# A two-block bottleneck network on 16 images: four first convolutions ahead of the first attention, weights prepared without ScalarE, and a new order of the 3x3 groups

## The chip, the cores and the metric

The kernel runs on one core of one Trainium2 chip. The metric is the device time of one execution in microseconds. "The time" of a kernel below is the median of its timed executions; a profile is one single execution, taken by the hardware profiler.

## The reference

The input is 16 images of 1024 channels and 32x32 pixels, in float32. Two residual bottleneck blocks follow each other. The first has local self-attention in its middle, the second a 3x3 convolution, computed by the Winograd method (inputs and weights are transformed, so that fewer multiplications are needed). Cut to what matters:

```python
# block 0
h = relu(bn(conv1x1(x, w_conv1)))                 # 1024 -> 256: "first convolution"
q = relu(bn(conv1x1(h, wq)))                      # "projections"
k = relu(bn(conv1x1(h, wk)))
v = bn(conv1x1(h, wv))
kp = unfold3x3(k) + pos                           # 9 taps, 32 heads of 8 channels
attn = softmax(einsum('bgdhw,bgdkhw->bgkhw', q, kp), axis=taps)
a = relu(bn(einsum('bgdkhw,bgkhw->bgdhw', unfold3x3(v), attn)))
x = relu(bn(conv1x1(a, w_conv3)) + x)             # 256 -> 1024: "third convolution"
# block 1
h = relu(bn(conv1x1(x, w1)))                      # 1024 -> 256: "reduction"
h = relu(bn(conv3x3(h, w2)))                      # "3x3 groups" (Winograd)
x = relu(bn(conv1x1(h, w3)) + x)                  # 256 -> 1024: "expansion"
```

## The kernel before

TensorE multiplies, ScalarE evicts PSUM (copies finished sums out of the accumulators, with scale, bias and relu), VectorE does the attention (products, sums over taps, weighted terms) and the Winograd transforms. The weights that stay the same are prepared once at the start and stored to device memory: two scaled 1x1 weights and the transformed 3x3 weights.

```python
def winograd_weights():
    for m in range(NW):                      # two halves
        ...                                  # three loads of u2t, issued by ScalarE
        for i, row in enumerate((g[0], mid[0], mid[1], g[2])):
            ...
            spread(lambda j: row[:, j, :], lambda j: u[:, j, :], WID)      # VectorE
            nc.scalar.activation(u[:, 0, :], row[:, 0, :], AF.Identity)
            nc.scalar.activation(u[:, 3, :], row[:, 2, :], AF.Identity)
            nc.scalar.dma_start(uw[i][:, m], u)
        yield
```

The attention of a later image is a generator, `side`, that is advanced a little after each piece of TensorE work; the number in `side.leave(us)` says how many us of VectorE work are let out there.

```python
def cycle(b, conv3):
    for o in conv3.chunks(take("w3", b), attended.pop(b), nothing):   # third convolution
        ...                                                           # residual loads
        side.leave(3.0)
    along(reduce_one(b), 3.0)                                         # reduction
    forms = transform(b)
    ...
    if 0 < b and b + 2 < B:                                           # first convolution of b + 2
        for c in first_conv(b + 2): ...
    for at, _ in enumerate(winograd_conv(b, forms, early)): ...       # 3x3 groups
    if more:
        for at in project(b + 2):                                     # projections of b + 2
            ...
            side.leave(3.0)
        side.start(attend(b + 2))
    ...
    for o in last.chunks(...):                                        # expansion
        nc.scalar.dma_start(out[b, ...], xr.pop((b, o)))
        if o >= BEHIND:                                               # BEHIND = 3
            load_residual(b + 1, o - BEHIND)
        if o == 4 and following:
            finish_attended(b + 1)                                    # relu of the attention's result
        side.leave(3.0)
```

So one image's turn is: third convolution, reduction, first convolution of the image two ahead, 3x3 groups, projections of the image two ahead, expansion. The 3x3 groups are sixteen pieces of eight matmuls; four accumulator tiles i = 0 to 3 get four pieces each, and ScalarE copies a tile's sum out after `first(i)` and again after `second(i)`, before the next piece may add to that tile.

```python
for part, i in (
    (first, 0), (third, 0), (first, 1), (second, 0), (third, 1), (last, 0), (second, 1),
    (first, 2), (third, 2), (last, 1), (second, 2), (first, 3), (last, 2), (second, 3),
    (third, 3), (last, 3),
):
```

Three times a piece follows on the same tile directly after a piece whose sum is being copied out: `(third, 0)` after `(first, 0)`, `(third, 2)` after `(first, 2)` and `(third, 3)` after `(second, 3)`. Everywhere else at least one piece of another tile lies between.

Of the kernel before, what the change touches and what calls it, by code (L numbers as in the profile page):

```python
# [13 lines left out]
P = 128  # L14
# [11 lines left out]
XSTREAM = 4  # L26
NJ = 4
# [34 lines left out]
def sa_bottleneck_kernel(ctx: ExitStack, tc: tile.TileContext, x, w1t, wqkvt, w3t, u1t, u2t, u3t, params, out):  # L62
# [17 lines left out]
    def load_x(b, c):  # L80

        if b < B:
            t = xpool.tile([P, HW], F32, tag="x", name=f"x_{b}_{c}")
            nc.gpsimd.dma_start(t, x[b, c * P : (c + 1) * P, :])
            xs[b, c] = t
# [17 lines left out]
    def fetch(name, b):  # L103

        t = wpool.tile([P, 2048], F32, tag="w", name=f"{name}_{b}")
        if name[0] == "U":
            i = int(name[1])
            nc.sync.dma_start(t, uw[i].rearrange("p m j o -> p (m j o)"))
            ready.append((name, b, t.rearrange("p (m j o) -> p m j o", m=NW, j=NU)))
            return  # L110
        if name in ("w3", "u3"):
            nc.sync.dma_start(t, ws[name == "u3"].rearrange("p n o -> p (n o)"))
            ready.append((name, b, t.rearrange("p (n o) -> p n o", n=NW)))
            return
        src, n = {"w1": (w1t, WID), "wqkv": (wqkvt, 3 * WID), "u1": (u1t, WID)}[name]
        chunks = src.shape[0] // P
        view = t[:, : chunks * n].rearrange("p (c n) -> p c n", n=n)
        nc.sync.dma_start(view, src.rearrange("(c p) n -> p c n", p=P))
        ready.append((name, b, view))
# [76 lines left out]
    def scaled_weights(which, src, scale):  # L196
        t = ppool.tile([P, NW, C], F32, tag="t", name="scaled")
        nc.scalar.dma_start(t, src.rearrange("(n p) o -> p n o", p=P))
        diag = ppool.tile([P, 2 * HW], F32, tag="t", name="diag")[:, :C]
        nc.vector.tensor_tensor(  # L200
            diag.rearrange("p (o m) -> p o m", m=P),
            eye.unsqueeze(1).to_broadcast([P, NC, P]),
            scale.unsqueeze(2).to_broadcast([P, NC, P]),
            ALU.mult,
        )
        row = psum.tile([P, C], F32, tag="ps", name="row")
        for half in range(2):
            nc.tensor.matmul(row[:, halves(half)], ones, diag[:, halves(half)], start=True, stop=True)
        for n in range(NW):
            nc.vector.tensor_tensor(t[:, n, :], t[:, n, :], row, ALU.mult)  # L210
        nc.scalar.dma_start(ws[which], t)
# [12 lines left out]
    def winograd_weights():  # L224
        for m in range(NW):
            g = []
            for i in range(3):
                t = rpool.tile([P, HW], F32, tag="r", name="g")[:, : 3 * WID]
                nc.scalar.dma_start(t, u2t[m * P : (m + 1) * P, i * 3 * WID : (i + 1) * 3 * WID])
                g.append(t)  # L230
            mid = [rpool.tile([P, HW], F32, tag="r", name="mid")[:, : 3 * WID] for _ in range(2)]
            spread(lambda i: g[i], lambda i: mid[i - 1], 3 * WID)
            for i, row in enumerate((g[0], mid[0], mid[1], g[2])):
# [4 lines left out]
                nc.scalar.activation(u[:, 0, :], row[:, 0, :], AF.Identity)  # L238
                nc.scalar.activation(u[:, 3, :], row[:, 2, :], AF.Identity)
                nc.scalar.dma_start(uw[i][:, m], u)  # L240
# [182 lines left out]
    def logits(b):  # L423
# [38 lines left out]
        se = apool.tile([P, JPIX], F32, tag="se", name="se")  # L462
# [82 lines left out]
    def winograd_conv(b, forms, early):  # L545
# [8 lines left out]
        def small(name, bufs=2):  # L554
            return zpool.tile([P, NW * TILES], F32, tag=name, name=name, bufs=bufs)
# [31 lines left out]
        def second(i):  # L587
# [3 lines left out]
            diffs[i] = small("d", 1)  # L591
# [25 lines left out]
        for part, i in (  # L617
            (first, 0), (third, 0), (first, 1), (second, 0), (third, 1), (last, 0), (second, 1),
            (first, 2), (third, 2), (last, 1), (second, 2), (first, 3), (last, 2), (second, 3),
            (third, 3), (last, 3),  # L620
        ):
            part(i)
            yield part, i
# [46 lines left out]
    BEHIND = 3  # L670

    def cycle(b, conv3):
# [9 lines left out]
        if 0 < b and b + 2 < B:  # L682
# [8 lines left out]
        more = b + 2 < B  # L691
        for at, _ in enumerate(winograd_conv(b, forms, early)):
            if not more and at in (12, 14):
                last.seed()
        if more:
            for at in project(b + 2):
                if at == ("bnk", 0):
                    finish_winograd(b)
                elif at == ("q", 1):
                    side.finish()  # L700
                    last.seed()
                elif at == ("bnv", 0):
                    last.seed()
                side.leave(3.0)
            side.start(attend(b + 2))
        else:
            side.finish()
            finish_winograd(b)
        following = last_conv(b + 1) if b + 1 < B else None
        for o in last.chunks(  # L710
# [5 lines left out]
            if o == 4 and following:  # L716
                finish_attended(b + 1)
            side.leave(3.0)
        return following


    queue += [("w1", 0), ("wqkv", 0), ("w1", 1), ("w1", 2), ("wqkv", 1)]
    for b in range(B):
        queue += [("w3", b), ("u1", b)]
        if 0 < b and b + 2 < B:
            queue.append(("w1", b + 2))
        queue += [(f"U{i}", b) for i in range(NU)]
        if b + 2 < B:
            queue.append(("wqkv", b + 2))
        queue.append(("u3", b))  # L730
# [7 lines left out]
    forms = winograd_weights()  # L738
    for c in first_conv(0):
        if c in (2, 4):  # L740
            next(forms)
    scaled_weights(0, w3t, col("L0_conv_bn3_s", 0, NC))
    scaled_weights(1, u3t, bn_inv[:, 2 * NW : 2 * NW + NC])
# [5 lines left out]
    along(first_conv(2), 3.4)  # L749
    conv3 = last_conv(0)  # L750
    for at in project(1):
        if at == ("q", 1):
            side.finish()
            conv3.seed()
        elif at == ("bnv", 0):
            conv3.seed()
        side.leave(3.4)
# [44 lines left out]
```

## Time and profile before

| | before |
|---|---|
| time, median of 3 runs | 2855.01 us (2852.85 to 2861.91) |
| profiled execution | span 2844.2 us, timed 2845.9 us |
| TensorE busy | 92% of the span, mean granted clock 0.969 |
| start to the first third convolution | 229.0 us |
| image 0, image 1, image 2 | 183.8, 166.4, 164.6 us |
| images 3 to 13, together | 1827.6 us (166.1 each) |
| images 14 and 15 to the end | 272.8 us |

The image rows are read from the trace: an image begins at the first matmul of its third convolution and ends at that of the next image. They cover the whole span, so two kernels can be compared stretch by stretch, and the differences add up exactly.

The first is the chain that ended last, around the end of the first attention (columns: start us, duration us, what):

```profile
212.74 4.00 DMA a<-acc
...
218.03 12.36 DMA a<-a
```

The attention's result is stored in 4.0 us and loaded again in the other layout in 12.4 us. The second is what TensorE waited for over images 3 to 13 (total us, times, longest us):

```profile
PE ps L299 <- ACT ps L290: 24.5, 18, 4.1
PE ps L568 <- ACT m L582: 15.8, 22, 0.7
PE ps L568 <- ACT m L590: 8.5, 11, 1.0
```

The first row is the expansion or third convolution waiting for its accumulator to be seeded with the residual; the other two are 3x3 groups (line 568) that wait for ScalarE to copy their tile out: 33 waits in 11 images, three per image.

### The profile page before, as it was taken

To read this page: it belongs to the slowest core of one execution; us is meant where nothing else is said; L and a number is where in the kernel's file an instruction comes from. 1 tells how busy PE (TensorE), PEld (TensorE's weight loads), DVE (VectorE), ACT (ScalarE), POOL (GpSimd) and SP (SyncE) were. 2 spreads that over 40 slices of the span, in tenths; PEclk is the share of its full clock that TensorE was granted. 3 is DMA by queue.
4 is the path that set the end of the run, shared out by engine and by line. 5 is a ranking of instruction groups with operands and counts; after the bars stand their busy time and mean duration, and the time that the engine had idled before them with its cause. 6 is when DMAs were issued, how large, how long until landed. Compare 5 with 4: busy or idle time off the path is not lost.

```text
span 2844.2 us, 19171 instructions
## 1 busy us (share of the span) xinstructions
PE 2626.0 (92%) x7048; PEld 1331.0 (47%) x7048; DVE 1945.2 (68%) x1693; ACT 949.3 (33%) x947; POOL 199.1 (7%) x363
## 2 busy tenths in 40 slices
PE   5767869999999999999999999999999999999888
PEld 2323524545454454545445454544545454454535
DVE  3676697496685949668593976859496685948703
ACT  1122231432515244251524425152442515143233
POOL 1100000000001000010100001010000101000000
PEclk8988979999999999999999999999999999999899
DMA  8843462645738264573826457382645738163332
GB/s 281 286 138 113 139 226 87 244 165 176 266 116 316 86 236 174 173 276 115 316 90 239 164 176 279 107 322 91 243 167 174 274 114 322 67 242 145 126 133 96
DMA packets 185358, 533.23 MB, mean 187 GB/s; under 512 B 12720, under 2 KB 102832, under 8 KB 164528
## 3 DMA queue, kind: packets, MB, share of 16 engines
q1 hardware_dynamic: 113152, 233.33, 23.8%
q0 software_dynamic: 50688, 220.75, 21.7%
q10 hardware_dynamic: 21424, 77.92, 6.9%
q8 instruction: 57, 0.93, 0.1%
q14 instruction: 37, 0.30, 0.0%
HBM read 372.03 MB, written 159.91 MB: 187 GB/s over the span
## 4 chain that ended last, share of the span: by engine, by line
PE 74%; DMA 17%; DVE 5%; ACT 2%; issue 1%; ACTq 0%; POOL 0%; SPq 0%; DVEq 0%; POOLq 0%
PE ps L268 30%; PE ps L299 17%; PE ps L568 16%; PE ps L351 10%; DMA u<-in_u1t_dram 8%; DMA bnv<-vh 3%; DMA r<-in_x_dram 3%; DVE term L478 2%; DVE acc L490 2%; PE ps L399 1%; DMA g<-in_u2t_dram 1%; ACT m L582 1%; DMA a<-a 1%; ACT ps L290 1%; ACT vh L361 0%
## 5 line engine op out<-in xcount | busy, mean ns | idle before, releaser
L430 DVE TENSOR_TENSOR prod<-qc,bnk 128x2048 f32<-128x2048 f32 x144 | 329.0, 2285 | 400.4 <-DMA qc<-q 400.3
L299 PE MATMUL ps<-a,w 128*128 128x512 f32 x1024 | 455.3, 605 | 78.2 <-ACT a L503 44.3
L568 PE MATMUL ps<-v,U 128*128 128x256 f32 x2048 | 468.3, 388 | 47.3 <-ACT m L582 23.0
L299 PE MATMUL ps<-h,u 128*128 128x512 f32 x1024 | 453.3, 603 | 42.2 <-ACT ps L290 35.6
L268 PE MATMUL ps<-x,w 128*128 128x512 f32 x1024 | 445.8, 596 | 28.7 <-DMA x<-in_x_dram 28.7
L568 PEld LDWEIGHTS ps<-v,U 128*128 128x128 f32 x2048 | 391.8, 193 | 128.4 <-ACT m L582 36.8
L268 PE MATMUL ps<-r,u 128*128 128x512 f32 x1024 | 442.1, 592 | 0.0
L299 PEld LDWEIGHTS ps<-a,w 128*128 128x128 f32 x1024 | 196.1, 193 | 337.2 <-issue 235.7
L351 PE MATMUL ps<-h,wqkv 128*128 128x512 f32 x768 | 337.0, 595 | 0.0
L299 PEld LDWEIGHTS ps<-h,u 128*128 128x128 f32 x1024 | 197.5, 194 | 294.8 <-issue 233.1
L268 PEld LDWEIGHTS ps<-x,w 128*128 128x128 f32 x1024 | 195.8, 191 | 275.6 <-issue 246.1
L268 PEld LDWEIGHTS ps<-r,u 128*128 128x128 f32 x1024 | 194.6, 190 | 244.9 <-issue 244.9
L290 ACT ACTIVATE ps<-r 128x1024 f32<-128x1024 f32 x256 | 261.8, 1023 | 134.8 <-DMA r<-in_x_dram 73.5
L490 DVE TENSOR_TENSOR acc<-acc,term 128x2048 f32<-128x2048 f32 x128 | 293.4, 2292 | 4.4
L478 DVE TENSOR_TENSOR term<-e,bnv 128x2048 f32<-128x2048 f32 x128 | 292.5, 2285 | 0.9
L351 PEld LDWEIGHTS ps<-h,wqkv 128*128 128x128 f32 x768 | 145.0, 190 | 183.9 <-issue 171.0
L308 ACT ACTIVATE r<-ps,par 128x1024 f32<-128x1024 f32 x128 | 142.2, 1111 | 174.2 <-PE ps L299 174.2
L433 DVE TENSOR_TENSOR prod<-prod 128x1024 f32<-128x1024 f32 x144 | 176.4, 1225 | 5.0
L308 ACT ACTIVATE r<-ps,bn_sh 128x1024 f32<-128x1024 f32 x128 | 141.7, 1107 | 85.0 <-PE ps L299 85.0
L322 ACT ACTIVATE h<-ps,par 128x1024 f32<-128x1024 f32 x32 | 38.4, 1204 | 393.2 <-PE ps L268 392.7
L537 DVE TENSOR_TENSOR v<-tv 128x512 f32<-128x512 f32 x256 | 160.0, 687 | 2.2
L532 DVE TENSOR_TENSOR tv<-vh 128x1088 f32<-128x1088 f32 x64 | 82.3, 1286 | 112.5 <-ACT vh L520 112.3
(83 smaller groups left out, 1286.1 us busy)
## 6 DMA issues: line engine op xcount, KB each, us to landing
x<-in_x_dram POOLq DMA_DIRECT2D x128, 512.0 KB, 3.8
r<-in_x_dram POOLq DMA_DIRECT2D x128, 512.0 KB, 8.1
U<-uw SPq DMA_DIRECT2D x64, 1024.0 KB, 4.8
out_dram<-r ACTq DMA_DIRECT2D x128, 512.0 KB, 8.1
bnk<-kp SPq DMA_DIRECT2D x32, 680.0 KB, 4.1
bnk<-bnk POOLq DMA_DIRECT2D x16, 1360.0 KB, 9.6
bnv<-vh SPq DMA_DIRECT2D x32, 680.0 KB, 10.4
bnv<-bnv POOLq DMA_DIRECT2D x16, 1360.0 KB, 9.7
```

Source lines behind the costliest of these rows:

```text
L268: nc.tensor.matmul(ps[n][:, halves(half)], wt[:, c, n * P : (n + 1) * P], src[:, halves(half)], start=(c == 0), stop=(c == NC - 1),)
L290: nc.scalar.activation(ps, xr[self.b, len(self.ahead)], AF.Identity)
L299: nc.tensor.matmul(ps[:, halves(half)], wt[:, n, o * P : (o + 1) * P], src[:, n, halves(half)], start=False, stop=(n == NW - 1), skip_grou ...
L308: nc.scalar.activation(xr[self.b, o], ps, RELU, bias=self.shift(o), scale=1.0)
L351: nc.tensor.matmul(ps[:, halves(half)], wqkv[:, m, at : at + P], h[:, m, halves(half)], start=(m == 0), stop=(m == NW - 1),)
L430: nc.vector.tensor_tensor(by_row(t), by_row(qc), kc[:, :, i : i + JROWS, j : j + W], ALU.mult)
L433: nc.vector.tensor_add(t[:, 0:4], t[:, 0:4], t[:, 4:8])
L478: nc.vector.tensor_tensor(by_row(dst), rows(e[:, k, :]).unsqueeze(1).to_broadcast([P, HEAD_DIM, JROWS, W]), vc[:, :, i : i + JROWS, j : j ...
L490: nc.vector.tensor_add(acc, acc, t)
L532: nc.vector.tensor_tensor(t, vh[:, :, i0 : i0 + 2 * NT - 1 : 2, :], vh[:, :, i1 : i1 + 2 * NT - 1 : 2, :], op)
L537: nc.vector.tensor_tensor(v[:, j].rearrange("p n (r w) -> p n r w", w=NT), t[:, :, :, j0 : j0 + 2 * NT - 1 : 2], t[:, :, :, j1 : j1 + 2 * ...
L568: nc.tensor.matmul(sums[i][:, at, n * TILES : (n + 1) * TILES], u[:, m, j, n * P : (n + 1) * P], v[:, j, m, :], start=(start and m == 0 an ...
```

## The change

The intent: fill TensorE while the first attention runs, by moving image 3's first convolution ahead of it, and with it take work out of image 1; prepare weights without ScalarE in the way; let no 3x3 group wait for a copy; load each residual one chunk behind the store that frees its buffer. In images 0 and 1 the projections of images 2 and 3 now come after the expansion instead of before it. Cut to its core:

```diff
+AHEAD = 4
     def winograd_weights():
...
-                nc.scalar.dma_start(t, u2t[...])
+                nc.sync.dma_start(t, u2t[...])
...
-                nc.scalar.activation(u[:, 0, :], row[:, 0, :], AF.Identity)
-                nc.scalar.activation(u[:, 3, :], row[:, 2, :], AF.Identity)
-                nc.scalar.dma_start(uw[i][:, m], u)
+                nc.vector.tensor_copy(u[:, 0, :], row[:, 0, :])
+                nc.vector.tensor_copy(u[:, 3, :], row[:, 2, :])
+                nc.sync.dma_start(uw[i][:, m], u)
...
         for part, i in (
-            (first, 0), (third, 0), (first, 1), (second, 0), (third, 1), (last, 0), (second, 1),
-            (first, 2), (third, 2), (last, 1), (second, 2), (first, 3), (last, 2), (second, 3),
-            (third, 3), (last, 3),
+            (third, 0), (first, 0), (third, 1), (second, 0), (first, 1), (last, 0), (second, 1),
+            (third, 2), (first, 2), (last, 1), (third, 3), (first, 3), (second, 2), (second, 3),
+            (last, 2), (last, 3),
         ):
...
-    BEHIND = 3
+    BEHIND = 1
...
-        if 0 < b and b + 2 < B:
+        if has_first(b):                       # AHEAD <= b + 2 < B
             for c in first_conv(b + 2):
...
-        more = b + 2 < B
+        more, late = b + 2 < B, b + 2 < AHEAD
...
-        if more:
-            for at in project(b + 2): ...
-            side.start(attend(b + 2))
+        if more and not late:
+            projections()                      # project(b + 2), then side.start(attend(b + 2))
...
         for o in last.chunks(...):
...
+        if late:
+            projections()
+            finish_attended(b + 1)
...
-    queue += [("w1", 0), ("wqkv", 0), ("w1", 1), ("w1", 2), ("wqkv", 1)]
+    queue += [("w1", 0), ("wqkv", 0), ("w1", 1), ("w1", 2), ("wqkv", 1), ("w1", 3)]
...
     along(first_conv(1), 3.4)
     along(first_conv(2), 3.4)
-    ...                                        # project(1) with side.leave(3.4)
+    along(project(1), 3.4)
+    along(first_conv(3), 3.4)
+    side.finish()
```

Beside these, the first four images' input loads go out from ScalarE instead of GpSimd, the scaled weights come before the Winograd weights and both before the first convolution, and the new group order gets a second buffer for its differences, paid for by letting the softmax sum share the maximum's buffer. The first `w1` is loaded in eight pieces instead of one.

More of the change, by code (lines that the diff above doesn't have):

```diff
@@ L83, in load_x @@
             t = xpool.tile([P, HW], F32, tag="x", name=f"x_{b}_{c}")
-            nc.gpsimd.dma_start(t, x[b, c * P : (c + 1) * P, :])
+            (nc.scalar if b < AHEAD else nc.gpsimd).dma_start(t, x[b, c * P : (c + 1) * P, :])
             xs[b, c] = t
@@ L117, in fetch @@
         view = t[:, : chunks * n].rearrange("p (c n) -> p c n", n=n)
-        nc.sync.dma_start(view, src.rearrange("(c p) n -> p c n", p=P))
+        src = src.rearrange("(c p) n -> p c n", p=P)
+        if b == 0 and name == "w1":
+            for c in range(chunks):
+                nc.sync.dma_start(view[:, c], src[:, c])
+        else:
+            nc.sync.dma_start(view, src)
         ready.append((name, b, view))
@@ L194, in sa_bottleneck_kernel, with scale_row @@
     )
-    def scaled_weights(which, src, scale):
-        t = ppool.tile([P, NW, C], F32, tag="t", name="scaled")
-        nc.scalar.dma_start(t, src.rearrange("(n p) o -> p n o", p=P))
+    def scale_row(scale):
         diag = ppool.tile([P, 2 * HW], F32, tag="t", name="diag")[:, :C]
@@ L208, in scaled_weights @@
             nc.tensor.matmul(row[:, halves(half)], ones, diag[:, halves(half)], start=True, stop=True)
+        return row
+    def scaled_weights(which, src, row):
+        t = ppool.tile([P, NW, C], F32, tag="t", name="scaled")
+        nc.sync.dma_start(t, src.rearrange("(n p) o -> p n o", p=P))
         for n in range(NW):
             nc.vector.tensor_tensor(t[:, n, :], t[:, n, :], row, ALU.mult)
-        nc.scalar.dma_start(ws[which], t)
+        nc.sync.dma_start(ws[which], t)
     def spread(g, dst, shape):
@@ L228, in winograd_weights @@
                 t = rpool.tile([P, HW], F32, tag="r", name="g")[:, : 3 * WID]
-                nc.scalar.dma_start(t, u2t[m * P : (m + 1) * P, i * 3 * WID : (i + 1) * 3 * WID])
+                nc.sync.dma_start(t, u2t[m * P : (m + 1) * P, i * 3 * WID : (i + 1) * 3 * WID])
                 g.append(t)
@@ L461, in logits @@
         yield 3.0
-        se = apool.tile([P, JPIX], F32, tag="se", name="se")
+        se = apool.tile([P, JPIX], F32, tag="mx", name="se")
         tree(ALU.add, se)
@@ L552, in winograd_conv, with small @@
         us, sums, firsts, diffs = {}, {}, {}, {}
-        def small(name, bufs=2):
-            return zpool.tile([P, NW * TILES], F32, tag=name, name=name, bufs=bufs)
+        def small(name):
+            return zpool.tile([P, NW * TILES], F32, tag=name, name=name, bufs=2)
         def by_tile(ap):
@@ L590, in second @@
             nc.scalar.activation(both, sums[i][:, 0], AF.Identity)
-            diffs[i] = small("d", 1)
+            diffs[i] = small("d")
             nc.vector.scalar_tensor_tensor(diffs[i], firsts[i], 2.0, both, ALU.mult, ALU.subtract)
@@ L690, in cycle, with projections @@
         last = expand_last(b)
-        more = b + 2 < B
+        more, late = b + 2 < B, b + 2 < AHEAD
         for at, _ in enumerate(winograd_conv(b, forms, early)):
-            if not more and at in (12, 14):
+            if (late or not more) and at in (12, 14):
                 last.seed()
-        if more:
+        def projections():
             for at in project(b + 2):
-                if at == ("bnk", 0):
+                if at == ("bnk", 0) and not late:
                     finish_winograd(b)
@@ L700, in cycle @@
                     side.finish()
-                    last.seed()
-                elif at == ("bnv", 0):
+                    if not late:
+                        last.seed()
+                elif at == ("bnv", 0) and not late:
                     last.seed()
@@ L705, in cycle @@
             side.start(attend(b + 2))
+        if more and not late:
+            projections()
         else:
-            side.finish()
             finish_winograd(b)
@@ L715, in cycle, with has_first @@
                 load_residual(b + 1, o - BEHIND)
-            if o == 4 and following:
+            if o == 4 and following and not late:
+                side.finish() if not more else None
                 finish_attended(b + 1)
             side.leave(3.0)
-        return following
-    queue += [("w1", 0), ("wqkv", 0), ("w1", 1), ("w1", 2), ("wqkv", 1)]
+        if late:
+            projections()
+            finish_attended(b + 1)
+        return following
+    def has_first(b):
+        return AHEAD <= b + 2 < B
+    queue += [("w1", 0), ("wqkv", 0), ("w1", 1), ("w1", 2), ("wqkv", 1), ("w1", 3)]
     for b in range(B):
         queue += [("w3", b), ("u1", b)]
-        if 0 < b and b + 2 < B:
+        if has_first(b):
             queue.append(("w1", b + 2))
         queue += [(f"U{i}", b) for i in range(NU)]
+        after = [("u3", b)]
         if b + 2 < B:
-            queue.append(("wqkv", b + 2))
-        queue.append(("u3", b))
+            after.insert(1 if b + 2 < AHEAD else 0, ("wqkv", b + 2))
+        queue += after
     load_x(0, 0)
@@ L737, in sa_bottleneck_kernel @@
     more_weights()
-    forms = winograd_weights()
-    for c in first_conv(0):
-        if c in (2, 4):
-            next(forms)
-    scaled_weights(0, w3t, col("L0_conv_bn3_s", 0, NC))
-    scaled_weights(1, u3t, bn_inv[:, 2 * NW : 2 * NW + NC])
+    scales = [scale_row(col("L0_conv_bn3_s", 0, NC)), scale_row(bn_inv[:, 2 * NW : 2 * NW + NC])]
+    scaled_weights(0, w3t, scales[0])
+    scaled_weights(1, u3t, scales[1])
+    for _ in winograd_weights():
+        pass
+    along(first_conv(0), 0.0)
     along(project(0), 0.0)
@@ L749, in sa_bottleneck_kernel @@
     along(first_conv(2), 3.4)
+    along(project(1), 3.4)
+    along(first_conv(3), 3.4)
+    side.finish()
     conv3 = last_conv(0)
-    for at in project(1):
-        if at == ("q", 1):
-            side.finish()
-            conv3.seed()
-        elif at == ("bnv", 0):
-            conv3.seed()
-        side.leave(3.4)
+    for _ in range(2):
+        conv3.seed()
     finish_attended(0)
```

## The prediction

> **What bounds the kernel now.** I read the page first, then busy time by stretches cut at the starts of the third convolutions, then the timelines of TensorE, VectorE and the issuing engines inside the stretches where TensorE is not full.
>
> The page: span, busy row, and TensorE's row of the 40 slices.
>
> ```profile
> span 2844.2 us, 19171 instructions
> PE 2626.0 (92%) x7048; PEld 1331.0 (47%) x7048; DVE 1945.2 (68%) x1693; ACT 949.3 (33%) x947; POOL 199.1 (7%) x363
> PE   5767869999999999999999999999999999999888
> ```
>
> TensorE is full from the seventh slice (about 430 us) on, apart from the tail. The change leaves its arithmetic alone, so it can win only in the head, in the few us that TensorE loses per image, and in the tail. Busy time by stretch: start-up, first attention, images 0 and 1, one steady image (columns: length, PE, PEld, DVE, ACT, POOL busy, clock, DMA share, GB/s).
>
> ```profile
> 0.00:98.00 98.00, 67.20 (x146) 28.38 (x147) 27.06 (x61) 17.72 (x27) 12.64 (x25) 0.90 0.81 280
> 98.00:229.00 131.00, 72.67 (x169) 31.17 (x167) 110.58 (x80) 19.38 (x16) 17.35 (x32) 0.79 0.62 213
> 229.00:413.00 184.00, 147.34 (x377) 75.37 (x378) 133.99 (x115) 54.43 (x55) 6.80 (x12) 0.86 0.38 133
> 413.00:579.00 166.00, 162.94 (x440) 82.74 (x440) 105.95 (x91) 58.40 (x58) 11.59 (x21) 0.99 0.54 193
> 1245.00:1411.00 166.00, 162.97 (x445) 82.91 (x444) 122.36 (x105) 59.17 (x59) 12.66 (x23) 1.00 0.56 200
> ```
>
> From 98 to 229 us VectorE is busy for 110.6 of 131 us: the first attention sets the pace. From 229 to 413 us image 0 takes 184 us for 147 of matmuls. Image 1 and the steady images, each with one first convolution inside, take 166. The timelines say what each stretch waits for.
>
> ```profile
> 71.49 2.35 DVE L210 TENSOR_TENSOR scaled<-scaled,row 128x1024 f32<-128x1024 f32 x2 [7.58 <-DMA scaled<-in_u3t_dram]
> 75.53 1.47 SPq L375 DMA_DIRECT2D bnk<-kp  x2
> 98.17 2.29 DVE L430 TENSOR_TENSOR prod<-qc,bnk 128x2048 f32<-128x2048 f32 x1 [24.33 <-DMA qc<-q]
> 167.36 1.22 DVE L449 TENSOR_TENSOR tree<-e 128x1024 f32<-128x1024 f32 x1 [18.32 <-ACT e L460]
> ...
> 228.96 2.08 PE L299 MATMUL ps<-a,w 128*128 128x512 f32 x2 [43.64 <-ACT a L503]
> 292.13 3.75 PE L568 MATMUL ps<-v,U 128*128 128x256 f32 x8 [4.08 <-issue]
> ...
> 1496.55 12.35 PE L568 MATMUL ps<-v,U 128*128 128x256 f32 x56 [0.69 <-ACT m L582]
> 1509.65 10.63 PE L568 MATMUL ps<-v,U 128*128 128x256 f32 x48 [0.75 <-ACT m L582]
> 1521.03 3.72 PE L568 MATMUL ps<-v,U 128*128 128x256 f32 x16 [0.75 <-ACT m L590]
> ...
> 1576.29 3.70 PE L299 MATMUL ps<-a,w 128*128 128x512 f32 x8 [1.42 <-ACT ps L290]
> ...
> 2671.48 26.27 PE L299 MATMUL ps<-h,u 128*128 128x512 f32 x56 [3.25 <-ACT h L630]
> ```
>
> The reader should see: weight preparation ends near 74 us and only then are k and q stored, so attention starts at 98; its exponential comes 18.3 us late, because ScalarE has it queued behind the first convolution that ends at 162.5; TensorE waits 43.6 us for the result. In a steady image the 3x3 groups lose 0.69+0.75+0.75 = 2.2 us, and seeding the sums with residuals a few us more. The waits of TensorE over 745 to 2400 us (ten images) sum to 22.4 us for seeds and 14.3+7.7 = 22.0 us for the groups: 2.2 us each per image.
>
> **What the Trainium skill says.** "TensorE: Matmul & The Clock Gate", Part 1, "What's actually happening": after an idle window of about 3.4 us the array falls to half clock and needs about as much busy time to recover. The trace agrees: clock 0.79 in the stretch with the 43.6 us wait, 1.00 in the steady one. "VectorE: DVE Perf Modes", the perf-mode tier table: float32 copies and tensor_scalar run at twice the rate of tensor_tensor. Here a 128x256 tensor_scalar took 0.28 us and a tensor_tensor 0.42, which sizes the new copies. "DMA: Bandwidth & Descriptors", "Issuing engines are not separate DMA queues": moving an issue saves sequencer time, not transfer time. The trace agrees: DMA is 0.81 busy in the first 98 us, whoever issues.
>
> **The change part by part.**
>
> Weight preparation. ScalarE is freed of 16 copies of about 0.4 us and of all waits behind them; VectorE gets 16 copies of 0.28, about 5 us in all with gaps. The chain itself stays serial, now on SyncE, which also stores k and q: whatever stands behind it waits as before. Link by link, with this trace's durations: the first scaled weight lands behind 5.7 MB of other loads at about 300 GB/s, near 20 us; its multiply 2.4; the second load 8 and multiply 2.4 (33.5); three loads of 3x3 weights about 10 (44.5); one half on VectorE 8.6+2.6 = 11.2 (56); the next loads 9 to 12 and its half 11.2: end about 76 to 78, against 74 before. The gain comes behind that: the first convolution and projection no longer wait on ScalarE, so k and q are ready and all four stores go out at once, the last at about 79 instead of 83.2. Attention then starts near 95 instead of 98.2.
>
> First attention. Logits and maximum: 98.2 to 149.0 is 51 us, so 146. Input loads leave GpSimd, so the 14.7 us gap of the second image's first convolution goes; the third one ends near 125 to 135 and the exponential no longer waits: 2.5 instead of 18.3 us. Sum, reciprocal and nine weighted terms: 167.4 to 212.7 is 45.3 us, so about 194. Store, load and relu took 16.3 us to the first matmul; with less behind it, 13 to 14. The third convolution of image 0 starts near 208, not 229: gain 21. The fourth first convolution (64 x 0.43 = 27.5 us) fits into the idle time before it, ending near 175.
>
> Images 0 and 1. Taking the first convolution out of image 1 helps only if TensorE bounds it. In the new order: third convolution 31.5 (cold clock), reduction 27.5, gap 4.1, groups 34.5-2.2 = 32.3, relu wait 3.3, to which 1.8 is added because the last two transform steps now both fall after the last group: expansion starts at 100.5. The exponential of the next attention is emitted after the second expansion chunk (the side schedule reaches it at 55.7 us of cost, with 3 per chunk and 16 chunks before): 9 us for two cold chunks, 1.6 for the relu, 2.6 for store and exponential, so 113.8. VectorE's tail 45.3 gives 159; store, load and relu 15 give 174. TensorE needs about 146 of it. So each of the two images takes 174: together 348, against 184+166 = 350. Gain 2: the moved convolution has only been replaced by waiting.
>
> Image 2. Its attention starts after the expansion instead of before it, so 24 us less of it is out before the transforms; seven terms (34 us) come after the groups. Their result lands near 163 and ScalarE, waiting for it at expansion chunk 4, delays the last chunk. About 170 instead of 166: loss 4.
>
> 3x3 groups. The three waits fall where a group follows on the same accumulator as one that ScalarE is copying out. In the new order another tile's group of 1.72 us always lies between, more than the 0.5+0.6 us of that copy. Images 3 to 13: 11 x 2.2 = 24. Images 14 and 15 are bounded by VectorE's order or expose the 1.8 us: 0.5 each, 1 together.
>
> Residuals. A residual load waits for its store to land, 12 us in the steady image, in either order, and nothing else of GpSimd's stands between. Effect about 0.
>
> Sum: 21 + 2 - 4 + 24 + 1 = 44 us.
>
> **The rivals.** (a) TensorE, not attention, bounds images 0 and 1, as the intent assumes. Then each takes about 150 and the gain is 44+48 = 92: 2763 us. For it: TensorE is 89 to 92% busy on average. Against: image 0 already took 184 us for 147 us of matmuls. (b) Input loads and weight preparation share [...]bandwidth; DMA is at 0.81. If the first convolution stalls on transfers queued behind preparation, attention starts 10 to 15 us later than before and most of the first gain goes: 2830 to 2840. (c) The residual order does help and removes the 2.2 us of seed waits over 13 images: 29 more, 2782. Against: each load's last release is the store. (d) The group waits are taken over by VectorE (a transformed tile is ready only 1 to 2 us before its group): 24 us lost, 2835.
>
> **Range and chances.** 2855 - 44 = 2811 us. Errors: start-up 8 to 10 us, images 0 to 2 about 12, steady images 10, profile against timed runs 5: together about 19, so 2784 to 2836. Two per cent faster means below 2798, 13 us beyond the centre: 0.25 with some weight on (a) and (c). Slower by 2% would need a new stall of 100 us: 0.02.
>
> **What would show it.** Right: TensorE's 0.7 us waits in the groups gone; steady images 163 to 164 us; first third convolution near 208; two waits of 20 to 40 us for the attention's result at the ends of images 0 and 1; the second attention's exponential inside the expansion. Wrong: images 0 and 1 near 150 us, steady images below 162, or first attention starting below 85 or above 105 us.

## More of the kernel before

The prediction shows the page and the timelines. Two views that it does not show are needed later.

## The result and the profile after

Ratios here are the mean time of one kernel's runs over the mean of the other's in the same rounds, so they are not quite the ratio of the medians that stand beside them.

| | before | changed |
|---|---|---|
| time, median, first comparison | 2858.25 us (4 runs) | 2813.37 us (4 runs, 2804.06 to 2818.23) |
| ratio, 95% interval | | 0.9841, 0.9808 to 0.9873 |
| the same again on another occasion | 2850.25 us (11 runs) | 2811.66 us (6 runs), 0.9862, 0.9835 to 0.9889 |
| profiled span | 2844.2 us | 2816.5 us |

The two profiles differ by 27.7 us, the timed medians by 39 to 45. The profiled execution of the kernel before was a quick one (2845.9 us, below all of its own timed runs of the first comparison), that of the changed kernel the slowest of its four (2818.2 us). Among the 33 later runs of the kernel before (medians 2846 to 2850 us) 2845.9 is an ordinary time. Stretch by stretch, with the prediction's amounts:

| stretch, us | before | changed | difference | predicted |
|---|---|---|---|---|
| start to the first third convolution | 229.0 | 216.3 | -12.7 | -21 |
| images 0 and 1 | 350.2 | 345.1 | -5.1 | -2 |
| image 2 | 164.6 | 180.0 | +15.4 | +4 |
| images 3 to 13 | 1827.6 | 1800.2 | -27.4 | -24 |
| images 14 and 15 to the end | 272.8 | 274.9 | +2.1 | -1 |
| whole | 2844.2 | 2816.5 | -27.7 | -44 |

The page of the changed kernel; its lines of code have moved by 11, so that line 568 is now 579 and line 299 is 310:

```profile
span 2816.5 us, 19073 instructions
PE 2622.3 (93%) x7048; PEld 1338.1 (48%) x7048; DVE 1949.5 (69%) x1709; ACT 944.3 (34%) x931; POOL 182.6 (6%) x331
PE   7968968799899999999999999999999999998788
```

The same 7048 matmuls, 4 us less of them busy: what moved is waiting. The dip in TensorE's row now reaches to the eleventh slice, about 770 us, where the row of before was full from the seventh. Busy time by stretch, cut at the starts of the third convolutions of images 0 to 3 and of one steady image (columns: length, PE, PEld, DVE, ACT, POOL busy, clock, DMA share, GB/s):

```profile
0.00:98.00 98.00, 76.22 (x170) 32.82 (x171) 31.80 (x77) 11.96 (x11) 6.29 (x13) 0.95 0.80 277
98.00:216.00 118.00, 90.39 (x207) 38.35 (x205) 109.24 (x79) 21.26 (x18) 11.00 (x20) 0.90 0.82 299
216.00:389.00 173.00, 140.41 (x377) 73.80 (x378) 121.79 (x104) 56.94 (x57) 7.94 (x14) 0.89 0.43 145
389.00:561.00 172.00, 140.96 (x376) 73.02 (x376) 117.75 (x102) 56.41 (x56) 7.91 (x14) 0.90 0.45 154
561.00:741.00 180.00, 167.02 (x440) 84.09 (x440) 133.60 (x115) 56.49 (x57) 10.56 (x20) 0.95 0.49 171
1231.00:1394.00 163.00, 160.43 (x440) 82.40 (x440) 118.30 (x103) 58.56 (x58) 12.16 (x22) 1.00 0.57 200
```

Images 0 and 1 now have 377 and 376 matmuls, 140 to 141 us of them, and still take 172 to 173 us. Image 2 takes 180 for 167. The steady image takes 163 for 160. TensorE's timeline says what the early images wait for (start, duration, work, idle time before it and what ended it):

```profile
216.25 29.22 PE L310 MATMUL ps<-a,w 128*128 128x512 f32 x64 [20.56 <-ACT a L514]
...
388.81 2.07 PE L310 MATMUL ps<-a,w 128*128 128x512 f32 x2 [22.54 <-ACT a L514]
...
561.37 30.84 PE L310 MATMUL ps<-a,w 128*128 128x512 f32 x64 [20.95 <-ACT a L514]
...
732.66 6.39 PE L310 MATMUL ps<-h,u 128*128 128x512 f32 x8 [7.98 <-ACT ps L301]
...
1479.77 27.79 PE L579 MATMUL ps<-v,U 128*128 128x256 f32 x128
1507.39 17.33 PE L362 MATMUL ps<-h,wqkv 128*128 128x512 f32 x40
```

Three times in a row the third convolution stands for 21 to 23 us until the relu of the attention's result (line 514) is done. VectorE is not full there either: it is busy for 122 of 173 us in image 0, and in the middle of that image's attention it waits 14.5 us for the exponential, which ScalarE has queued behind evictions of the expansion:

```profile
326.74 1.23 DVE L460 TENSOR_TENSOR tree<-e 128x1024 f32<-128x1024 f32 x1 [14.54 <-ACT e L471]
```

So "the attention" below means its whole chain (VectorE's work, the exponential's place on ScalarE, stores and loads), not VectorE's capacity. In image 2 the last chunk of the expansion waits 8 us for a seed. And the 3x3 groups of a steady image, 128 matmuls, run in one piece.

### The profile page after: what moved, and what is told of

Its sections match the earlier page's. It is cut to its first block, busy times and chain, and to the rows that moved or that the text cites. A ratio compares the mean times of both kernels' runs of the same rounds, so it can differ in the third digit from the quotient of the medians.

```text
span 2816.5 us, 19073 instructions
## 1 busy us (share of the span) xinstructions
PE 2622.3 (93%) x7048; PEld 1338.1 (48%) x7048; DVE 1949.5 (69%) x1709; ACT 944.3 (34%) x931; POOL 182.6 (6%) x331
## 3 DMA queue, kind: packets, MB, share of 16 engines
q0 software_dynamic: 46080, 203.97, 20.6%
## 4 chain that ended last, share of the span: by engine, by line
PE 70%; DMA 16%; DVE 10%; issue 2%; ACT 2%; SPq 0%; POOL 0%; ACTq 0%; DVEq 0%; POOLq 0%
PE ps L279 27%; PE ps L310 18%; PE ps L579 16%; PE ps L362 8%; DMA u<-in_u1t_dram 4%; DMA bnv<-vh 3%; DMA r<-in_x_dram 3%; DVE term L489 3%; DVE acc L501 3%; DMA a<-a 1%; PE ps L410 1%; DMA a<-acc 1%; DVE prod L441 1%; ACT ps L301 1%; DMA g<-in_u2t_dram 1%
## 5 line engine op out<-in xcount | busy, mean ns | idle before, releaser
L310 PE MATMUL ps<-a,w 128*128 128x512 f32 x1024 | 462.4, 613 | 93.6 <-ACT a L514 64.8
L579 PE MATMUL ps<-v,U 128*128 128x256 f32 x2048 | 455.2, 385 | 25.3 <-issue 24.9
```

The costliest lines, as they stand in the source:

```text
L310: nc.tensor.matmul(ps[:, halves(half)], wt[:, n, o * P : (o + 1) * P], src[:, n, halves(half)], start=False, stop=(n == NW - 1), skip_grou ...
L579: nc.tensor.matmul(sums[i][:, at, n * TILES : (n + 1) * TILES], u[:, m, j, n * P : (n + 1) * P], v[:, j, m, :], start=(start and m == 0 an ...
```

## The experiments

The theory after reading the two traces: the group order is worth nearly the whole gain, and more than its visible waits; the moved first convolution is worth nothing, because images 0 and 1 are paced by the attention; the start-up gains 13 us, which image 2 gives back. The rivals: that the start-up carries the gain; that TensorE's work bounds images 0 and 1, so that the moved convolution pays; that the residual order pays. Each kernel was timed in five rounds against the kernel before on the same chip. The runs were made on three chips; where ratios are compared below, the changed kernel's two (0.9841 and 0.9862) show how well such a ratio repeats.

**The group order alone.** The kernel before, with the new order and the buffers that it needs.

```diff
-            (first, 0), (third, 0), (first, 1), (second, 0), (third, 1), (last, 0), (second, 1), ...
+            (third, 0), (first, 0), (third, 1), (second, 0), (first, 1), (last, 0), (second, 1), ...
-        se = apool.tile([P, JPIX], F32, tag="se", name="se")
+        se = apool.tile([P, JPIX], F32, tag="mx", name="se")
-            diffs[i] = small("d", 1)
+            diffs[i] = small("d")
```

> The kernel before with only the 3x3 group order of the change and the buffers that it needs (two difference tiles; the sum shares the maximum's tile). Theory: the three waits of 0.7 us on ScalarE's copies vanish in every image, 2.2 us each; about 26 us over the images that TensorE bounds, so a ratio of 0.990 to 0.992 and waits of TensorE on those copies near 0 (before: 24 us over images 3 to 13). Rival: VectorE takes the waits over, because both last steps of the transform come after the last group: ratio 0.998 or more and new waits of the same size.

Measured: 2796.63 us against 2846.05, ratio 0.9828 (0.9792 to 0.9865): 49 us, nearly twice what was expected, and no less than the whole change gives. The waits of this kernel over the whole span have no row for a 3x3 group that waits for a copy. The early images gain too: images 0 to 2 took 179.4, 161.0 and 161.8 us, against 183.8, 166.4 and 164.6. That it is the order and not the buffers is shown by the next kernel, which keeps the buffers.

**All but the group order.** The changed kernel with the old order.

```diff
-            (third, 0), (first, 0), (third, 1), ...
+            (first, 0), (third, 0), (first, 1), (second, 0), (third, 1), (last, 0), (second, 1), ...
```

> The changed kernel with the group order of before and all the rest kept. Theory: the rest of the change (start-up, four first convolutions ahead, residuals) is worth about 12 us at the first attention and loses 10 us in images 0 to 2, so the time is within 8 us either way of 10 us under before: ratio 0.994 to 0.999. Rival: the convolutions ahead carry the gain: ratio 0.985 to 0.990, and images 0 to 2 stay as they are in the changed kernel (172, 173, 180 us) either way.

Measured: 2849.63 us against 2846.05, ratio 1.0006 (0.9973 to 1.0038): no gain, just past the expected 0.994 to 0.999. The waits that return, whole span (total us, times, longest):

```profile
PE ps L579 <- ACT m L593: 22.9, 32, 0.7
...
PE ps L579 <- ACT m L601: 12.0, 16, 0.7
```

That is 48 waits, three in each of 16 images, 34.9 us together. Their removal is worth 49 us in the first experiment and, between this kernel's ratio and the changed kernel's two, 41 to 47 us (0.0144 to 0.0165 times 2846; each ratio is good to some 9 us). So a visible wait of 0.7 us seems to cost more than 0.7 us.

**The residual order.** The changed kernel with `BEHIND = 3` as before.

> The changed kernel with residual loads three chunks behind the stores, as before. Theory: each load still waits for its own store to land and nothing else stands between on GpSimd, so the same time within 4 us as the changed kernel (ratio to before 0.983 to 0.987), seed waits over images 3 to 13 about 25 us as in both profiles. Rival: the order is worth the 2.2 us of seed waits per image: 25 us slower than the changed kernel.

Measured: 2812.77 us against 2846.05, 0.9870 (0.9835 to 0.9905), images 3 to 13 1799.9 us against the changed kernel's 1800.2. Seed waits in images 3 to 13 are 28.0 us here, 25.6 in the changed kernel and 24.5 before. The residual order has no effect that these runs can see.

**Attention let out faster in the early images.** If the attention paces images 0 and 1, letting more of its work out during the third convolution and the reduction should shorten them.

```diff
-            side.leave(3.0)
-        along(reduce_one(b), 3.0)
+            side.leave(4.2 if b + 2 <= AHEAD else 3.0)
+        along(reduce_one(b), 4.2 if b + 2 <= AHEAD else 3.0)
```

> The changed kernel with the attention's work emitted faster in images 0, 1 and 2: 4.2 instead of 3.0 us per chunk in the third convolution and the reduction, so that the exponential and the first terms come before the transform. Theory: the attention's place in the order sets images 0 and 1 (172.5 us each for some 150 of TensorE) and the late end in image 2 (180): they fall to about 151, 151 and 164, together 58 us, ratio to before 0.962 to 0.970. Rival: TensorE or transfers set them: they stay at 172, 172, 180 and the ratio at 0.984.

Measured: 2778.32 us against 2846.05, ratio 0.9761 (0.9727 to 0.9794). No matmul was removed and the kernel is about 1% quicker than the changed one, so TensorE's work does not bound these images. But the expected ratio (0.962 to 0.970) was missed: image 0 fell from 172.6 to 156.8 us (151 expected), image 1 took 169.3 (151 expected) and image 2 172.8 (164 expected). For image 1, VectorE's timeline has the reason:

```profile
377.24 2.29 DVE L441 TENSOR_TENSOR prod<-qc,bnk 128x2048 f32<-128x2048 f32 x1 [34.83 <-DMA qc<-q]
```

VectorE stood for 34.8 us because q of image 2 had only just been projected: with the projections behind the expansion, an attention that ends early only waits for the next one's input. The groups of image 1 then came late for their transform, which stood behind the attention's work on VectorE:

```profile
449.99 30.56 PE L579 MATMUL ps<-v,U 128*128 128x256 f32 x128 [19.41 <-issue]
```

**The fourth convolution back in image 1.**

```diff
-AHEAD = 4
+AHEAD = 3
-    ..., ("wqkv", 1), ("w1", 3)]
+    ..., ("wqkv", 1)]
-    along(first_conv(3), 3.4)
```

> The changed kernel with three first convolutions ahead instead of four; the fourth goes back into image 1, whose projection then comes before its expansion again. Theory: in the changed kernel TensorE only waits in the time that the moved convolution freed, so nothing is lost by putting it back: start of the first third convolution near 216 us as in the changed kernel, image 0 about 172, image 1 about 180 (as image 2 of the changed kernel: its attention starts late), image 2 about 165, so some 8 us less than the changed kernel; ratio to before 0.980 to 0.985. Rival: the convolution ahead is worth its 27 us of TensorE: 20 us or more slower than the changed kernel, ratio 0.991 or more.

Measured: 2794.48 us against 2848.28, ratio 0.9806 (0.9778 to 0.9834), as expected. `AHEAD = 3` also brings the projections of image 3 before the expansion of image 1 again. Images 0 to 2 take 511.5 us here (169.8, 180.8, 161.0) and 525.1 in the changed kernel. Moving the convolution ahead did not help; with its projections moved behind the expansion in image 1 it costs about 14 us by the profiles and 10 to 16 by the ratios, whose intervals overlap. The idle time before the first third convolution grew by 23 us, most of the 27.5 us of the convolution that left it:

```profile
211.06 29.83 PE L310 MATMUL ps<-a,w 128*128 128x512 f32 x64 [43.70 <-ACT a L514]
```

It is 43.7 us here and 20.6 in the changed kernel, yet the start moved by only 5 us, and to the earlier side.

**The loads of the weight preparation first.** In the changed kernel the chain of preparation runs on SyncE in order: load, multiply, store, load, and so on. Here the loads that depend on nothing go out ahead of the stores that wait.

```diff
+    loaded = [scaled_load(w3t), scaled_load(u3t)]
+    first_half = winograd_load(0)
-    scaled_weights(0, w3t, scales[0])
-    scaled_weights(1, u3t, scales[1])
-    for _ in winograd_weights():
+    scaled_weights(0, loaded[0], scales[0])
+    scaled_weights(1, loaded[1], scales[1])
+    for _ in winograd_weights(first_half):
```

> The changed kernel with the loads of the two scaled weights and of the first half of the 3x3 weights issued before the first store of a prepared weight. Theory: the serial chain load, multiply, store, load on SyncE is what k and q wait behind; it ends near 57 us instead of 74, attention starts near 88 instead of 102.7, the first third convolution near 202 instead of 216, the time falls by 12 to 15 us; ratio to before 0.979 to 0.983. Rival: transfers are the limit of the start-up (DMA 0.8 busy), so the order of their issue moves nothing: attention starts at 100 or later.

The mechanism is right: the last store of the preparation goes out at about 59 us instead of 74, the attention starts at 88.7 instead of 102.7, the first third convolution at 203.0 instead of 216.3:

```profile
88.73 2.29 DVE L448 TENSOR_TENSOR prod<-qc,bnk 128x2048 f32<-128x2048 f32 x1 [29.68 <-DMA qc<-q]
...
203.00 30.67 PE L317 MATMUL ps<-a,w 128*128 128x512 f32 x64 [21.16 <-ACT a L521]
```

The time is not: 2805.4 us against 2848.28, ratio 0.9845 (0.9818 to 0.9872), where 0.979 to 0.983 was expected; it is not told apart from the changed kernel's 0.9841 and 0.9862. Those two less the 13 us of the start would be 0.980 to 0.982, at the lower end of the interval. The profile is 13 us shorter (2803.4 against 2816.5); as a measurement of time this run is inconclusive.

**Projections before the expansion again, and the attention let out faster.** The order of before in images 0 and 1, with the fourth convolution still ahead.

```diff
-        more, late = b + 2 < B, b + 2 < AHEAD
+        more, late = b + 2 < B, False
-            after.insert(1 if b + 2 < AHEAD else 0, ("wqkv", b + 2))
+            after.insert(0, ("wqkv", b + 2))
-            side.leave(3.0)
-        along(reduce_one(b), 3.0)
+            side.leave(4.2 if b + 2 < AHEAD else 3.0)
+        along(reduce_one(b), 4.2 if b + 2 < AHEAD else 3.0)
```

> The changed kernel with the projections of images 2 and 3 before the expansions of images 0 and 1, as in the kernel before, and in those two images 4.2 us of attention emitted per chunk instead of 3.0. Theory: the late projection starts the next attention late, and with it before the expansion TensorE bounds both images: about 150 us each instead of 172.5, and image 2 about 164 instead of 180, because its attention starts before the expansion again; 50 to 60 us less than the changed kernel, ratio to before 0.963 to 0.968. Rival: attention or the residual loads set them all the same: 165 us or more each, ratio 0.978 or more.

Measured: 2753.24 us against 2848.28, ratio 0.9665 (0.9630 to 0.9699), as expected. Images 0 to 2 take 156.5, 151.4 and 160.6 us. Earlier projections without the faster letting-out were not tried with the convolution ahead. The wait at the end of image 0 is gone:

```profile
370.78 27.73 PE L310 MATMUL ps<-a,w 128*128 128x512 f32 x64 [2.80 <-ACT ps L301]
```

2.8 us for a seed, where the changed kernel waits 22.5 for the attention. This is what the change was after.

**Both together: the fastest version.** The last two edits in one kernel.

> The two edits of the two runs before together (loads of weights first; early projection with faster emission). Theory: they act in different stretches and add: 65 to 75 us less than the changed kernel, ratio to before 0.957 to 0.963, first third convolution near 202 us, images 0 and 1 about 150. Rival: an attention that starts earlier only waits elsewhere: no better than the early projection alone.

Measured: 2743.93 us (2734.22 to 2753.65) against 2848.28, ratio 0.9629 (0.9601 to 0.9657), correct, span of the profile 2732.5 us. It beats both kernels: 106 us under the one before by its ratio (0.0371 x 2848.28), 60 to 66 us under the changed one (0.0212 to 0.0233). The ratio is inside the expected range at its upper end; the first third convolution starts at 206.0 us (202 expected), images 0 and 1 take 155 each.

**The changed kernel again.**

> The changed kernel as it is, again, beside the next two and with more rounds, because its first ratio rested on three. Expected: 0.985, within 0.982 to 0.988. It tells the size of the whole change on the chip of the last experiments; if it is under 0.980 or over 0.990 the comparisons across chips above are not safe.

Measured: 2811.66 us against 2850.25, ratio 0.9862 (0.9835 to 0.9889), as expected.

**The fastest version with the old group order.**

> The fastest version so far (weights loaded first, early projection) with the group order of before. In it TensorE bounds nearly every image. Theory: each image's group stage is 3.0 us longer with the old order (0.7 us of wait three times[...]: 30.6 against 27.6 us in the profiles), so 14 to 16 images lose 3.0: 42 to 48 us more than the fastest, ratio to before 0.977 to 0.981. If only the 2.2 us of visible waits count: 31 to 35 us more, ratio 0.973 to 0.975.

Measured: 2791.99 us against 2850.25, ratio 0.9799 (0.9765 to 0.9832). Against 0.9629 that is 0.0170 x 2850 = 48 us for the group order, 3.0 per image, as in the first experiment (49). The waits that are visible are again only 35 us:

```profile
PE ps L586 <- ACT m L600: 23.0, 32, 0.7
...
PE ps L586 <- ACT m L608: 12.0, 16, 0.7
```

**The fastest version with the fourth convolution back in image 1.**

> The fastest version so far with the fourth first convolution put back into image 1. Theory: now that the attention no longer sets images 0 and 1, the 27.5 us convolution is worth its time ahead of the first result: 20 to 27 us more than the fastest version, ratio to before 0.969 to 0.973, image 1 about 162 to 180 instead of 151 to 155. Rival: it is worth nothing in any order, as in the changed kernel, where putting it back saved time: ratio 0.963 or less.

Measured: 2752.46 us against 2850.25, ratio 0.9664 (0.9634 to 0.9695). The expectation (0.969 to 0.973) was missed: the convolution is worth at most some 10 us, and the intervals overlap. In the traces, start to the third convolution of image 3 is 682.6 us with it back and 679.1 with it ahead: 3.5 us. With it ahead the first third convolution starts 5.3 us later (206.0 against 200.7), and image 1 of the fastest version is only 8 us shorter (154.9 against 163.2), because the hole that the convolution leaves is not filled:

```profile
433.69 30.17 PE L586 MATMUL ps<-v,U 128*128 128x256 f32 x128 [14.67 <-issue]
```

The groups wait 14.7 us for their transform, which stands behind the attention's work on VectorE, and 10.4 us before that VectorE itself was idle, because the exponential was queued on ScalarE behind evictions of the third convolution:

```profile
391.37 1.22 DVE L467 TENSOR_TENSOR tree<-e 128x1024 f32<-128x1024 f32 x1 [10.37 <-ACT e L478]
```

Even there, then, the attention sets the pace, by its place in the order more than by VectorE's capacity. A better place for the exponential was not tried.

## Why the prediction was right or wrong

The time was right: 2811 us predicted, 2813 and 2812 measured. The sum was right partly because its errors cancel, and three of its terms were mis-sized.

**Start-up, 21 us predicted, 12.7 measured: too much.** Three links of this step held. The preparation ended at about 74 us, as early as before, on SyncE (76 to 78 predicted), with 16 copies of 0.286 us on VectorE (0.28 predicted), and the attention's exponential no longer waits behind a first convolution. The row that answers to the 18.3 us of before, and the start of the attention ahead of it:

```profile
102.67 2.29 DVE L441 TENSOR_TENSOR prod<-qc,bnk 128x2048 f32<-128x2048 f32 x1 [28.86 <-DMA qc<-q]
...
155.73 1.23 DVE L460 TENSOR_TENSOR tree<-e 128x1024 f32<-128x1024 f32 x1 [2.19 <-ACT e L471]
```

What failed is "all four stores go out at once, the last at about 79 ... Attention then starts near 95". They did go out close together, and they landed late. The transfers issued between 60 and 100 us (columns: how many, KB each, median us from issue to landing), first before:

```profile
bnk<-kp SPq DMA_DIRECT2D x2, 680.0 KB, 5.8
...
q<-q SPq DMA_DIRECT2D x2, 512.0 KB, 4.8
...
qc<-q POOLq DMA_DIRECT2D x1, 1024.0 KB, 8.4
```

and then changed:

```profile
bnk<-kp SPq DMA_DIRECT2D x2, 680.0 KB, 10.8
...
q<-q SPq DMA_DIRECT2D x2, 512.0 KB, 12.2
qc<-q POOLq DMA_DIRECT2D x1, 1024.0 KB, 11.4
```

The store and load of q together took 12.2 + 11.4 = 23.6 us instead of 4.8 + 8.4 = 13.2. The chain to the attention's start runs through these two, so those 10 us are why it came at 102.7, not at 95 and not even at 98.2. That the crowd slowed them is read from the views, not isolated by a run: between 74 and 92 us the DMA share is 1.00 at 302 GB/s, and SyncE issues a 1 MB weight load (`w`, at 74.25 us) and all stores of k, q and v but the last v within 8 us; the weight load had been issued before 44 us in the kernel before. This is akin to rival (b) of the prediction, with a smaller delay (4.5 us later than before, not 10 to 15). The step from the attention's result to the first matmul came out near its size: store 9.1, load 4.2, relu 1.3 us, 15 in all, where 13 to 14 was predicted.

**Images 0 and 1, 174 us each predicted, 172.6 each measured: right, with the mechanism.** In image 0 the expansion began 97.3 us in (100.5 predicted), the exponential was done at 110.5 (113.8), VectorE at 155.8 (159). The second attention's exponential fell inside the expansion, and the waits of 22.5 and 21.0 us for the attention's result are those that the prediction named. That the moved convolution was "only replaced by waiting" is shown by three runs: images 0 to 2 are no slower with it back (511.5 us against 525.1), quicker when only the attention is let out earlier, and 21 us quicker in image 1 (172.6 to 151.4) once its projections come first and the attention is let out faster. Rival (a), TensorE as the bound, is false for the changed kernel; its 150 us per image came only with those two other edits.

**Image 2, a loss of 4 us predicted, 15.4 measured: the mechanism right, the size off.** The prediction had the attention's result landing near 163 us into the image and ScalarE waiting for it. It came at 727 to 730, 166 to 169 us into it, but it was not the only wait. ScalarE's timeline:

```profile
700.69 1.02 ACT L418 ACTIVATE by_offset<-ps 128x1024 f32<-128x1024 f32 x1 [7.51 <-DVE acc L501]
...
716.46 1.03 ACT L301 ACTIVATE ps<-r 128x1024 f32<-128x1024 f32 x1 [5.50 <-DMA a<-acc]
...
727.36 1.24 ACT L514 ACTIVATE a<-a,par 128x1024 f32<-128x1024 f32 x1 [6.36 <-DMA a<-a]
```

ScalarE stands 7.5 us for a buffer that the attention's sum (line 501) still holds, then 5.5 us for the result's store, then 6.4 us for its load: 19 us in which it evicts nothing and seeds nothing. TensorE, in expansion and third convolution, waits 1.8, 0.9, 8.0 and 2.3 us for seeds. Only the last of these three ScalarE waits was in the prediction's sum. That the late projections are the cause is supported by two versions that move image 3's projections before the expansion of image 1: 160.6 us with the attention also let out faster in images 0 and 1, 161.0 at the old pace with the convolution back in image 1. Letting out faster alone gave 172.8. The projections were never moved by themselves.

**3x3 groups, 2.2 us per image predicted, 3.0 measured: the mechanism right, the unit wrong.** The waits are gone as predicted (24.3 us in images 3 to 13 before, 0 after; the one group wait left there, 0.4 us, is for weights). But the visible idle time understates the loss. In a steady image the groups began at 1493.97 us and the projections after them at 1524.58 before, and at 1479.77 and 1507.39 in the changed kernel: 30.61 against 27.62 us for the same 128 matmuls, 3.0 us for three waits, so 1.0 us for a wait shown as 0.7. The clock was not the reason; the busy time of the stretch of before has it at 1.00 (the column before the DMA share):

```profile
1493.97:1524.58 30.61, 28.43 (x129) 24.07 (x128) 16.46 (x24) 7.24 (x11) 0.53 (x1) 1.00 0.41 148
```

The same stretch of the changed kernel:

```profile
1479.77:1507.39 27.62, 27.62 (x129) 24.32 (x128) 14.19 (x21) 7.26 (x11) 0.53 (x1) 1.00 0.39 131
```

So of the 3.0 us the profile books 2.2 as idle and 0.8 as busy time of the same matmuls. And this is no single image: from the first matmul of the groups to the projections, a steady image takes 30.6 us on average in all three profiles with the old order and 27.6 to 27.7 in all ten with the new one.

3.0 us in 16 images is 48 us, which is what the group order is worth on the kernel before (49) and on the fastest version (48). In the changed kernel images 0 to 2 are bounded elsewhere, so 11 steady images should give 33; 27.4 are in the profile. The groups did give theirs; about 7 us came back in the expansion, which took 28.8 us per steady image before and 29.5 in the changed kernel. That stage and the third convolution wait for seeds, and nearly all scatter between profiles lies in them: images 3 to 13 together take 1784 to 1809 us in the ten profiles with the new order and 1820 to 1828 in the three with the old one. Where the extra 0.3 us per wait goes inside TensorE is not settled by these runs.

**Residuals, 0 predicted, 0 measured**, shown by the run with `BEHIND = 3`. **The end, a gain of 1 us predicted, a loss of 2.1 measured**, within what single profiles scatter.

So the start-up was overrated by 8 us, image 2 underrated by 11, the groups underrated by 3 to 9, images 0 and 1 underrated by 3, and the end was 3 off. The profile pair moved by 28 us, not 44; the timed runs by 39 to 45. So the agreement of 44 with the timed runs should not be read as each term being right: it is partly luck. The most telling pair of numbers is another: the group order alone 0.9828, all the rest 1.0006.

## What to carry to other kernels

Before work is moved away from an engine, ask what sets the pace of that stretch: here TensorE was relieved of 27 us in an image that the attention's chain paced, and the time was spent waiting. No engine was full there (VectorE was busy for 122 of 173 us); what helped was letting the attention out faster, and most when its inputs came sooner as well. A short wait in a stream of matmuls should be priced by the distance from start to start against an unbroken stream, not by the idle time that the profile shows. And when an issuer is freed, check what now goes out together: the stores of q took 12.2 us to land, not 4.8.

## What the Trainium skill lacked or had wrong

- "TensorE: Matmul & The Clock Gate", "A second HAM failure mode: psum-queue depth-cycling", puts the loss from short stops between groups of matmuls down to the clock gate throttling again and again. Here three stops of 0.7 us in an image cost 3.0 us with the granted clock at 1.00 in that stretch, so the clock gate is not needed for such a loss. The page gives a matmul outside a stream a fixed latency on top of its columns; it does not say what a stop inside a stream costs beside the idle time that a profile shows (here 1.0 us for 0.7).
- "DMA: Bandwidth & Descriptors", "Issuing engines are not separate DMA queues", says that another issuer saves only issue time. The runs agree, but the page does not warn that freeing an issuer can bunch transfers: the stores of q took 12.2 us to land when they went out with their neighbours, and 4.8 when ScalarE's later evictions had spread them (the cause read from the views, not isolated by a run).
